# Output projection of two attention layers as seven products of halves, with its weights loaded into the place of the value weights

## The chip, the cores and the metric

The kernel runs on one NeuronCore of one Trainium2 chip. Five engines work side by side, each through its own queue of instructions in a fixed order: TensorE (PE in the profile, its weight loads PEld) multiplies matrices, VectorE (DVE), ScalarE (ACT) and GpSimd (POOL) work element by element, and SyncE (SP) issues most transfers (DMA). An instruction that has to wait holds up everything behind it in its own queue. Matrix products land in PSUM, eight banks of 128 x 512 float32 numbers; GpSimd takes no part in emptying them here, so VectorE and ScalarE carry every result out.

The metric is the device time of one execution, in microseconds (us): from the first to the last of the program's work, one launch.

## What is computed

Four layers in a row act on x of shape (2, 512, 32, 32), all in float32. Only the last two are touched by the change. Layers 2 and 3 are plain self-attention blocks over 1024 positions with 8 heads of 64 channels:

```python
xn = group_norm(x)                              # 8 groups in layer 2, 32 in layer 3
q, k, v = split(W_qkv @ xn + b_qkv)             # (2, 512, 1024) each
a = softmax(q.T @ k / 8) ; h = a @ v            # for each of 8 heads
x = x + W_proj @ h + b_proj                     # W_proj is 512 x 512
```

The two samples of the batch are called b = 0 and b = 1. Layer 0 (attention over sampled keys and an MLP) and layer 1 (linear attention) come before and take most of the time.

## The kernel before

x stays in SBUF through the whole program as eight tiles `x[b][t]` of 128 channels by 1024 positions (t = 0 to 3). Each of layers 2 and 3 is one call of `attention`, in three stages.

**Queries, keys, values** (`queries_keys_values`). The products with W_qk and W_v are made by Winograd's form of Strassen's scheme: both matrices are cut in four blocks, and seven products of block sums (P1 to P7, table `SEVEN`) take the place of eight. The sums of the weights (`left_sums`, four element-wise operations, on GpSimd) stand in a second tile beside the raw weights; the sums of the other side come from `right_sums`. A small comparison at the end, `oki`, says whether all logits are small, and every engine branches on it: with these inputs into `heads_bounded`.

**Heads** (`heads_bounded`). A unit is one sample b, one pair of heads p and one half h of the 512 + 512 query positions: 16 units of 8 steps, one step n for 128 keys. In a step, `score` makes four products into a score tile `s` (two banks, two buffers), ScalarE takes the exponential into `e` (six buffers), and `value`, two steps later, multiplies `e` with the values into the unit's result `o`. For the divisor the eight `e` are added up: three adds on GpSimd into `some`, the others on VectorE into `sum`. After a unit's last step ScalarE and VectorE carry `o` out of its banks into the queries' place (`q`), and four steps later `divide` makes the column sums `d` of `sum` on TensorE, takes the reciprocal on VectorE, multiplies, and adds the values' bias.

Only TensorE's order is written out by hand in this stage; the order of the other engines is what the framework's scheduler makes of the dependences. `o` and `d` have one place of two banks each. So the next unit may not start its `o` before the last one is carried out, and TensorE's hand-written order makes room for that: no `value` in the third step of a unit, two in the fourth (`for j in ([], [i - 3, i - 2])[i % NB == 3] if i % NB in (2, 3) else [i - 2]`).

**Projection** (end of `heads_bounded`, `project_block`, L591 to L609). For each sample and each block o of 128 output channels, eight products of 128 x 128 by 128 x 512 fill two banks `pb`, and two VectorE operations (L607) add the bias and the result to x. The last unit's `divide` stands after the first block. In layer 3 each half goes out at once with a DMA on SP's queue (L609). In layer 2 the statistics for layer 3's norm (`channel_means`, `group_means`) are taken in between, and the norm's first block (`norm_first`) is made before the last block.

The projection's weights are four tiles, loaded by SP after the branch (`projection_weights`, L943). The next layer's W_qk and W_v are loaded by SP as soon as the last value product of this layer has read the old ones. GpSimd has no work in the projection; in layer 2 it makes the sums of layer 3's W_qk in that time.

Of the kernel before, what the change touches and what calls it, by code (L numbers as in the profile page):

```python
# [11 lines left out]
F32 = mybir.dt.float32  # L12
# [40 lines left out]
class Net:  # L53
# [539 lines left out]
    def project_block(self, acc, att, w, bias: str, b: int, o: int, out):  # L593

        nc = self.nc
        for h in range(2):
            for t in range(CT):
                nc.tensor.matmul(  # L598
                    acc[:, h, :],
                    lhsT=w[t][:, o * P : (o + 1) * P],  # L600
                    rhs=att[t][:, h * HF : (h + 1) * HF],
                    start=(t == 0),
                    stop=(t == CT - 1),
                )
        for h in range(2):
            xt = self.xs[b][o][:, h * HF : (h + 1) * HF]
            nc.vector.scalar_tensor_tensor(xt, acc[:, h, :], self.col(bias, o), xt, ALU.add, ALU.add)  # L607
            if out is not None:
                nc.sync.dma_start(out[b, o][:, h * HF : (h + 1) * HF], xt)  # L609
# [321 lines left out]

    def attention_weights(self, pool, k: int):

        got = []
        for name in ("qk", "v"):
            src = self.io[f"l{k}_{name}"]
            got.append(pool.tile(list(src.shape), F32, tag=name, name=f"{name}w{k}"))
            self.nc.sync.dma_start(got[-1], src)  # L940
        return got

    def projection_weights(self, pool, k: int):  # L943
        got = []
        for t in range(CT):
            got.append(pool.tile([P, C], F32, tag=f"proj{t}", name=f"proj{k}{t}"))
            self.nc.sync.dma_start(got[-1], self.io[f"l{k}_proj"][t])
        return got

    def averages(self):  # L950
# [2 lines left out]
            self.avg[k] = self.norm.tile([P, P], F32, tag="avg", name=f"avg{k}")  # L953
            self.nc.sync.dma_start(self.avg[k], self.io[f"l{k}_avg"])

    def attention(self, k: int, weights, out, meanwhile=lambda: None):


        nc = self.nc
        with ExitStack() as ctx:  # L960
            one = self.pool(ctx, f"a{k}")
            ones = one.tile([P, DH], F32, tag="ones", name=f"ones{k}")
            nc.vector.memset(ones, 1.0)
            data = []
            for b in range(B):
                qs = [one.tile([P, N], F32, tag=f"q{b}{t}", name=f"q{k}{b}{t}") for t in range(CT)]
                ks = [one.tile([P, N], F32, tag=f"k{b}{t}", name=f"k{k}{b}{t}") for t in range(CT)]
                v = [one.tile([P, 2, C], F32, tag=f"v{b}{n}", name=f"v{k}{b}{n}") for n in range(NB // 2)]
                data.append((qs, ks, v))
            small_logits, got = self.queries_keys_values(k, weights, ones, data, meanwhile)  # L970
            if k == 2:
                self.means_tiles(3, 0)
                self.first[3] = self.first_block(3, 0)

            with self.tc.If(small_logits > 0) as cmp:
                self.heads_bounded(k, ones, data, out)
            with cmp.Else():
                self.heads_general(k, data)
                with ExitStack() as ctx2:
                    proj = self.projection_weights(self.pool(ctx2, f"a{k}_w_p"), k)  # L980
                    ps = self.pool(ctx2, f"a{k}_ps_p", 2, psum=True)
                    for b in range(B):
                        for o in range(CT):
                            acc = ps.tile([P, 2, HF], F32, tag="ps", name=f"pbg{k}{b}{o}")
                            self.project_block(acc, data[b][0], proj, f"pb{k}", b, o, out)
                    if k == 2:
                        for t in range(CT):
                            self.channel_means(3, 0, t)
                        for _ in self.group_means(3, 0, ps.tile([P, 2, HF], F32, tag="ps", name="gm3g")):
                            pass  # L990
                        self.norm_first(3)
            return got

    def queries_keys_values(self, k, weights, ones, data, meanwhile):

# [5 lines left out]
        with ExitStack() as ctx:  # L1003
# [133 lines left out]
                            for c in range(2):  # L1137
                                self.norm_block(k, 1, xns[1][i], i, c, act)
            with self.tc.manual_schedule(engines={mybir.EngineType.SP}):
                got = meanwhile()  # L1140
                reason = "a product of two comparisons"
                return nc.values_load(oki, min_val=0, max_val=1, skip_runtime_bounds_check_because=reason), got

    def largest(self, k, b, ones, cm, small, ps_g, flag):

# [71 lines left out]
        for c in range(2):  # L1217
            self.norm_block(k, 0, self.first[k], 0, c, (self.nc.vector, self.nc.scalar)[c])

    def heads_bounded(self, k, ones, data, out):  # L1220

# [2 lines left out]
        nc = self.nc  # L1226
        halves = [slice(0, DH), slice(DH, P)]
        with ExitStack() as ctx:
            proj = self.projection_weights(self.pool(ctx, f"b{k}_w"), k)
            ep = self.pool(ctx, f"b{k}_e", 6)  # L1230
            ap = self.pool(ctx, f"b{k}_a", 1)
            ap2 = self.pool(ctx, f"b{k}_a2", 2)
            ps_s = self.pool(ctx, f"b{k}_ps_s", 2, psum=True)
            ps_o = self.pool(ctx, f"b{k}_ps_o", 1, psum=True)

            def score(unit, n):
                b, p, h, state = unit
# [1 line left out]
                cut = slice(h * HF, (h + 1) * HF)  # L1239

                third = unit is units[0] and n == 2
                s = (ps_o if third else ps_s).tile([P, 2, HF], F32, tag="sd"[third], name=f"s{k}{b}{p}{h}{n}")
                for par, rows in enumerate(halves):
                    for c in range(2):
                        at = n * P + c * DH
# [20 lines left out]
            def value(unit, n):  # L1266
                b, p, h, state = unit
                v = data[b][2]
                if n == 0:
                    state["o"] = ps_o.tile([P, 2, HF], F32, tag="o", name=f"o{k}{b}{p}{h}")  # L1270
                o, e = state["o"], state["e"][n]
                for r, rows in enumerate(halves):
                    for par in range(2):
# [12 lines left out]

            def divide(unit):
                b, p, h, state = unit
                d = ps_o.tile([P, 2, HF], F32, tag="d", name=f"d{k}{b}{p}{h}")
                for r, rows in enumerate(halves):  # L1290
                    for par in range(2):
                        nc.tensor.matmul(
# [7 lines left out]
                nc.vector.tensor_tensor(res, res, t, ALU.mult)  # L1300
                nc.vector.tensor_scalar(res, res, self.col(f"vb{k}", p), None, ALU.add)

            units = [(b, p, h, {}) for b in range(B) for p in range(CT) for h in range(2)]
            steps = [(unit, n) for unit in units for n in range(NB)]
            with self.tc.manual_schedule(engines={mybir.EngineType.PE}):


                for i in range(len(steps) + 5):
                    if i < len(steps):
                        score(*steps[i])  # L1310
                    for j in ([], [i - 3, i - 2])[i % NB == 3] if i % NB in (2, 3) else [i - 2]:
                        if 0 <= j < len(steps):
                            value(*steps[j])
                    if i % NB == 4 and NB < i < len(steps):
                        divide(steps[i - NB][0])
                for b in range(B):
                    for o in range(CT):
                        acc = ps_s.tile([P, 2, HF], F32, tag="s", name=f"pb{k}{b}{o}")
                        self.project_block(acc, data[b][0], proj, f"pb{k}", b, o, out)
                        if b == o == 0:  # L1320
                            divide(units[-1])
                        if k == 2:
                            n = b * CT + o
                            if 1 <= n <= CT:
                                self.channel_means(3, 0, n - 1)
                            elif n == CT + 1:
                                steps = self.group_means(3, 0, ps_o.tile([P, 2, HF], F32, tag="d", name="gm3"))
                                next(steps)
                            elif n == CT + 2:
                                next(steps, None)  # L1330
                                self.norm_first(3)

    def heads_general(self, k, data):
        with ExitStack() as ctx:
# [78 lines left out]
def conv_seq_kernel(ctx: ExitStack, tc: tile.TileContext, io: dict[str, bass.AP], out: bass.AP):  # L1413
# [3 lines left out]
    with tc.tile_pool(name="w_at", bufs=1) as wpool, tc.tile_pool(name="norm", bufs=2) as norm:  # L1417
        net.norm = norm
        with tc.tile_pool(name="w_l1", bufs=1) as lpool:
            net.mlp0()  # L1420
            l1 = net.layer1_weights(lpool)
            l2 = net.attention_weights(wpool, 2)
            net.averages()
            net.layer1(*l1)
        l3 = net.attention(2, l2, None, lambda: net.attention_weights(wpool, 3))
        net.attention(3, l3, out.rearrange("b (t p) h w -> b t p (h w)", p=P))

# [7 lines left out]
def _blocks(w):  # L1437

    return np.ascontiguousarray(w.T).reshape(-1, P, w.shape[0])
# [38 lines left out]
def _layout(i):  # L1478
# [10 lines left out]
    def over(v):  # L1489
# [33 lines left out]
        "l1_b": np.concatenate([l1["bv"], l1["bq"], l1["bk"]]),  # L1523
        "l2_qk": _slabs(l2["qkv_w"][: 2 * C].T.reshape(1, C, 1, 2 * C))[0],
        "l2_v": _slabs(l2["qkv_w"][2 * C :].T.reshape(1, C, 1, C))[0],
        "l2_proj": _blocks(l2["proj_w"]),
        "l2_avg": _average(C // 8),
        "l3_qk": _slabs(w3[: 2 * C].T.reshape(1, C, 1, 2 * C))[0],
        "l3_v": _slabs(w3[2 * C :].T.reshape(1, C, 1, C))[0],
        "l3_proj": _blocks(l3["w_proj"]),  # L1530
        "l3_avg": _average(C // 32),
    }

# [15 lines left out]
```

## Time and profile before

| | us |
|---|---|
| median of 4 runs (3453.45 to 3454.75) | 3454.61 |
| the profiled execution | 3454.33 |
| its span, first to last instruction | 3452.5 |
| layers 0 and 1, and layer 2's queries, keys and values | 0 to 2704.5 |
| layer 2: heads / projection and way into layer 3 | 240.4 / 58.4 |
| layer 3: queries, keys and values | 147.9 |
| layer 3: heads / projection and end | 240.1 / 61.2 |

The stages are read from the timeline: the first score product of layer 2 starts at 2704.56 us, the first projection product at 2944.91, the first product of layer 3 at 3003.32, its heads at 3151.66 and its projection at 3391.28. TensorE is busy for 98% of the span, at a mean granted clock of 0.997. Lines of the profile read: start, duration, engine, line of the code, operation, output <- inputs, and in square brackets the idle time before it with what ended it. The profile counts every float32 product as two matrix records.

### The profile page before, as it was taken

Reading aid. Unit: us, or ns where it says so; the run is one execution under the profiler, and the core shown is the slowest. Engines: PE = TensorE matmul, PEld = TensorE weight load, DVE = VectorE, ACT = ScalarE, POOL = GpSimd, SP = SyncE. Lnnn points to the kernel's source line nnn. Section 1 sums busy time; section 2 is a strip of 40 time slices with the busy share of each in tenths; the row PEclk is TensorE's granted clock in tenths of the full one; section 3 lists DMA queues with packets and bytes.
Section 4 is the critical chain, followed back from the end, with each engine's and each line's share of the span. In section 5 each row is a group of like instructions: output and inputs, shape, how many; then the busy total and the mean of one; then the engine's idle time right before and its main releaser. Section 6 shows DMA issues by size and latency. Waiting matters only on the chain.

```text
span 3452.5 us, 60119 instructions
## 1 busy us (share of the span) xinstructions
PE 3397.1 (98%) x25280; PEld 1263.3 (37%) x25280; DVE 2314.5 (67%) x2539; ACT 2021.0 (59%) x2100; POOL 2080.1 (60%) x1584
## 2 busy tenths in 40 slices
PE   6999999999999999999999999999999999999999
PEld 2333333333333333333333334444555433455333
DVE  6877777777777567767776664575556577555774
ACT  5877877877887577877887761111111466113661
POOL 4778777787787577787788874342323444234441
PEclk9999999999999999999999999999989999999999
DMA  5778777777887577777788872111000100000001
GB/s 152 157 141 157 150 154 148 155 158 143 156 162 144 105 157 151 155 154 146 163 169 160 158 151 79 49 37 37 1 1 0 50 1 1 1 0 13 2 1 50
DMA packets 103247, 342.64 MB, mean 99 GB/s; under 512 B 12720, under 2 KB 14384, under 8 KB 100144
## 3 DMA queue, kind: packets, MB, share of 16 engines
q0 software_dynamic: 73296, 266.90, 40.9%
q1 hardware_dynamic: 28656, 69.68, 6.5%
q8 instruction: 202, 3.31, 0.4%
q10 hardware_dynamic: 1008, 2.06, 0.2%
q14 instruction: 85, 0.70, 0.1%
HBM read 67.27 MB, written 4.46 MB: 21 GB/s over the span
## 4 chain that ended last, share of the span: by engine, by line
PE 80%; DVE 15%; ACT 2%; POOL 1%; issue 1%; DMA 0%; DVEq 0%; ACTq 0%; SPq 0%; POOLq 0%
PE hp L486 46%; DVE h L455 3%; PE pb L598 3%; DVE r L1298 3%; PE sim L518 3%; PE o L1275 2%; DVE sum L1262 2%; PE s L1246 2%; PE qk20P L1041 1%; PE qk30P L1041 1%; PE m_0P L649 1%; PE qk31P L1041 1%; PE m_6P L649 1%; PE m_4P L649 1%; PE m_3P L649 1%; PE m_1P L649 1%
## 5 line engine op out<-in xcount | busy, mean ns | idle before, releaser
L486 PE MATMUL hp<-h,w 128*32 128x512 f32 x16384 | 1832.7, 593 | 5.4 <-DVE h L455 3.6
L455 DVE CUSTOM_DVE_ANT_1 h<-tx,bank 128x1024 f32<-128x1024 f32 x1024 | 1180.9, 1216 | 332.4 <-PE hp L486 309.3
L491 ACT ACTIVATE h<-hp,magb 128x1024 f32<-128x1024 f32 x1024 | 1124.0, 1113 | 416.2 <-PE hp L486 415.2
L486 PEld LDWEIGHTS hp<-h,w 128*32 128x32 f32 x16384 | 545.3, 110 | 1215.4 <-issue 1118.7
L478 POOL DMA_DIRECT2D h<-h x509 | 452.6, 1026 | 391.9 <-ACT h L497 334.6
L504 POOL TENSOR_TENSOR h<-h,h 128x1024 f32<-128x1024 f32 x255 | 613.7, 2407 | 21.3
L502 POOL TENSOR_SCALAR h<-h,flip 128x1024 f32<-128x1024 f32 x256 | 448.4, 1751 | 0.9 <-ACT h L491 0.9
L1250 ACT ACTIVATE e<-s 128x1024 f32<-128x1024 f32 x256 | 258.7, 1025 | 177.1 <-PE s L1246 164.4
L493 ACT ACTIVATE h<-h,flip 128x1024 f32<-128x1024 f32 x256 | 291.9, 1140 | 0.0
L1275 PE MATMUL o<-e,v 64*64 64x512 f32 x2048 | 261.0, 592 | 6.7 <-DVE q L1285 6.7
L1246 PE MATMUL s<-q,k 64*64 64x512 f32 x2048 | 259.8, 589 | 2.6 <-DVE v L1079 1.8
L1257 POOL TENSOR_TENSOR some<-some,e 128x1024 f32<-128x1024 f32 x64 | 151.5, 2367 | 75.7 <-ACT e L1250 73.4
L495 POOL TENSOR_SCALAR h<-h,flip 128x1024 f32<-128x1024 f32 x128 | 145.3, 1135 | 78.2 <-ACT h L491 77.0
L1255 POOL TENSOR_TENSOR some<-e,e 128x1024 f32<-128x1024 f32 x32 | 75.5, 2361 | 190.8 <-DVE sum L1264 155.6
L497 ACT ACTIVATE h<-h,flip 128x1024 f32<-128x1024 f32 x128 | 145.8, 1139 | 0.0
L518 PE MATMUL sim<-h,ends 128*32 128x512 f32 x1024 | 141.2, 592 | 0.0
L1260 DVE TENSOR_TENSOR sum<-e,e 128x1024 f32<-128x1024 f32 x32 | 46.3, 1448 | 136.1 <-ACT e L1250 136.1
L1275 PEld LDWEIGHTS o<-e,v 64*64 64x64 f32 x2048 | 75.7, 133 | 157.4 <-issue 123.7
L1246 PEld LDWEIGHTS s<-q,k 64*64 64x64 f32 x2048 | 78.5, 133 | 143.5 <-issue 116.6
L628 POOL TENSOR_TENSOR mlp_w<-mlp_w 128x512 f32<-128x512 f32 x16 | 22.5, 1405 | 160.7 <-DMA mlp_w<-in_mlp_w 106.4
L708 ACT ACTIVATE mh<-mh,cols 128x512 f32<-128x512 f32 x64 | 46.3, 724 | 124.1 <-DVE mh L726 65.4
L1029 POOL TENSOR_TENSOR sq<-q 128x512 f32<-128x512 f32 x32 | 33.3, 1039 | 139.3 <-DVE q L1048 95.2
(456 smaller groups left out, 3283.1 us busy)
## 6 DMA issues: line engine op xcount, KB each, us to landing
h<-h POOLq DMA_DIRECT2D x509, 512.0 KB, 6.5
lb<-logs SPq DMA_DIRECT2D x63, 512.0 KB, 5.2
mlp_w<-in_mlp_w SPq DMA_DIRECT2D x16, 1024.0 KB, 4.9
x<-in_x SPq DMA_DIRECT2D x8, 512.0 KB, 8.8
qkw<-in_l_qk SPq DMA_DIRECT2D x2, 2048.0 KB, 8.1
out<-x SPq DMA_DIRECT2D x16, 256.0 KB, 2.1
vw<-in_l_v SPq DMA_DIRECT2D x2, 1024.0 KB, 7.5
proj<-in_l_proj SPq DMA_DIRECT2D x8, 256.0 KB, 5.2
```

What stands on the lines that cost most here:

```text
L455: self.nc.vector._custom_dve(TENSOR_ADD_SAT, out=h[:, k, :, :], in0=x[:, jj, 2 * r + k, :].unsqueeze(1).to_broadcast([P, H, W]), in1=y[:, ...
L478: nc.gpsimd.dma_start(to, what, accum_op=ALU.add)
L486: nc.tensor.matmul(hp[rows, cut], lhsT=self.l0w2[:, 32 * q : 32 * q + 32], rhs=h1[k][:, cut], start=True, stop=True)
L491: nc.scalar.activation(y, hp, AF.Relu, bias=self.magb[:, q : q + 1])
L493: nc.scalar.activation(ys[0], ys[0], AF.Copy, scale=self.flip[:, 0:1])
L502: nc.gpsimd.tensor_scalar(y, y, self.flip[:, 2:3], 1.0, ALU.mult, ALU.mult)
L504: (nc.vector if final else nc.gpsimd).tensor_tensor(y, y, ys[2], ALU.add)
L518: nc.tensor.matmul(sims[u][at : at + 32, :], lhsT=self.ends[:, 28 - 4 * o : 60 - 4 * o], rhs=z[jj][:, h * HF : (h + 1) * HF], start=(o == ...
L649: self.nc.tensor.matmul(acc[p], lhsT=w[:, a, k, p * P : (p + 1) * P], rhs=right(r, k), start=k == 0, stop=k == 1)
L1246: nc.tensor.matmul(s[halves[c], par, :], lhsT=ks[p][rows, at : at + DH], rhs=qs[p][rows, cut], start=True, stop=True)
L1250: nc.scalar.activation(e, s, AF.Exp, scale=DH**-0.5)
L1275: nc.tensor.matmul(o[halves[par], r, :], lhsT=v[n // 2][rows, n % 2, at : at + DH], rhs=e[rows, par, :], start=(n == 0), stop=(n == NB - 1),)
```

## The change

In layers 2 and 3:

- The projection is made by the seven products too, per sample 28 products of 128 x 128 by 128 x 512 where there were 32. Its weights come in the layout of the other raw weights, one tile of 1 MB, with `left_sums` on GpSimd (`project_left`). The sums of the other side (`project_right`) are eight subtractions of 128 x 512 per sample: all on GpSimd for b = 0, half on GpSimd and half on VectorE for b = 1. They stand in buffers of `e`. The results are gathered as in the MLP: per sample 14 VectorE operations and 2 ScalarE copies that read PSUM, and 6 adds on GpSimd (L1334 of the new code).
- The projection's weights take the buffer of the value weights. SP loads them before the branch, once the last value product has read the old ones; layer 3's value weights are loaded after layer 2's projection.
- `o` and `d` of a unit share one place of two banks, and there are two such places, taken in turn by h. TensorE's order has one `value` in every step, always two steps behind.
- The last unit's `divide` stands after the third product (P1, P3, P2) of sample 0. The statistics for layer 3's norm are taken during sample 1, with `group_means` after its fourth and fifth product.

```diff
-    def projection_weights(self, pool, k: int):
-        ...
+    def attention_weights(self, pool, k: int, name: str):
+        src = self.io[f"l{k}_{name}"]
+        tag = "qk" if name == "qk" else "v"
+        got = pool.tile(list(src.shape), F32, tag=tag, name=f"{name}w{k}")
+        self.nc.sync.dma_start(got, src)
         return got
...
             with self.tc.manual_schedule(engines={mybir.EngineType.SP}):
-                got = meanwhile()
+                got = self.attention_weights(wpool, 3, "qk") if k == 2 else None
+                proj = self.attention_weights(wpool, k, "proj")
                 reason = "a product of two comparisons"
...
-            proj = self.projection_weights(self.pool(ctx, f"b{k}_w"), k)
+            wp = self.pool(ctx, f"b{k}_w", 1)
...
+            ps_even = self.pool(ctx, f"b{k}_ps_e", 1, psum=True)
             ps_s = self.pool(ctx, f"b{k}_ps_s", 2, psum=True)
-            ps_o = self.pool(ctx, f"b{k}_ps_o", 1, psum=True)
+            ps_odd = self.pool(ctx, f"b{k}_ps_o", 1, psum=True)
+
+            def place(h, name):
+                return (ps_even, ps_odd)[h].tile([P, 2, HF], F32, tag="o", name=name)
...
-                    state["o"] = ps_o.tile([P, 2, HF], F32, tag="o", name=f"o{k}{b}{p}{h}")
+                    state["o"] = place(h, f"o{k}{b}{p}{h}")
...
-                d = ps_o.tile([P, 2, HF], F32, tag="d", name=f"d{k}{b}{p}{h}")
+                d = place(h, f"d{k}{b}{p}{h}")
...
+            def project_left():
+                more = wp.tile([P, 3, 2, 2 * P], F32, tag="proj", name=f"projm{k}")
+                self.left_sums(nc.gpsimd, proj, more)
+                return [proj[:, i] for i in range(4)] + [more[:, i] for i in range(3)]
+
+            def project_right(b):
+                att = data[b][0]
+                r = [[att[2 * (i // 2) + c][:, (i % 2) * HF : (i % 2 + 1) * HF] for c in range(2)] for i in range(4)]
+                t = [ep.tile([P, 2, HF], F32, tag="e", name=f"pt{k}{b}{i}") for i in range(4)]
+                t1, t2, t3, t4 = ([x[:, c, :] for c in range(2)] for x in t)
+                for c in range(2):
+                    eng = nc.vector if b == 1 and c == 0 else nc.gpsimd
+                    eng.tensor_tensor(t1[c], r[1][c], r[0][c], ALU.subtract)
+                    eng.tensor_tensor(t2[c], r[3][c], t1[c], ALU.subtract)
+                    eng.tensor_tensor(t3[c], r[3][c], r[1][c], ALU.subtract)
+                    eng.tensor_tensor(t4[c], r[2][c], t2[c], ALU.subtract)
+                return [r[0], t3, r[2], r[3], t1, t2, t4]
...
+                for which in ("P1", "P3", "P2", "P6", "P7", "P5", "P4"):
+                    a, ri = SEVEN[which]
...
+                    acc = place(0, name) if which in ("P2", "P5") else ps_s.tile([P, 2, HF], F32, tag="s", name=name)
+                    for p in range(2):
+                        for c in range(2):
+                            nc.tensor.matmul(acc[:, p, :], lhsT=left[a][:, c, p * P : (p + 1) * P],
+                                rhs=right[ri][c], start=c == 0, stop=c == 1)
+                    for p in range(2):
...
+                        if which == "P1":
+                            nc.scalar.copy(u, got)
+                            add(vec, p, 0, got, True)
+                        elif which == "P3":
+                            add(vec, p, 1, got, True)
+                        elif which == "P2":
+                            add(vec, p, 0, got)
+                            store(p, 0)
+                        elif which == "P6":
+                            vec.tensor_tensor(u, got, u, ALU.add)
+                        elif which == "P7":
+                            vec.tensor_tensor(u3, got, u, ALU.add)
+                            add(pool, p, 3, u3)
+                            add(pool, p, 2, u3)
+                        elif which == "P5":
+                            vec.tensor_tensor(u, got, u, ALU.add)
+                            add(pool, p, 1, u)
+                            store(p, 1)
+                            add(vec, p, 3, got, True)
+                            store(p, 3)
+                        else:
+                            add(vec, p, 2, got, True)
+                            store(p, 2)
...
-                for i in range(len(steps) + 5):
+                for i in range(len(steps) + 2):
                     if i < len(steps):
                         score(*steps[i])
-                    for j in ([], [i - 3, i - 2])[i % NB == 3] if i % NB in (2, 3) else [i - 2]:
-                        if 0 <= j < len(steps):
-                            value(*steps[j])
+                    if i >= 2:
+                        value(*steps[i - 2])
                     if i % NB == 4 and NB < i < len(steps):
                         divide(steps[i - NB][0])
-                for b in range(B):
-                    for o in range(CT):
-                        ...
+                    if i == len(steps) // 2 + NB:
+                        left = project_left()
+                right = project_right(0)
+                for n, _ in enumerate(project(0, left, right)):
+                    if n == 2:
+                        divide(units[-1])
+                        right = project_right(1)
+                for n, _ in enumerate(project(1, left, right)):
+                    if k == 2:
+                        if n < 2:
+                            self.channel_means(3, 0, 2 * n)
+                            self.channel_means(3, 0, 2 * n + 1)
+                        elif n == 3:
+                            means = self.group_means(3, 0, place(1, "gm3"))
+                            next(means)
+                        elif n == 4:
+                            next(means, None)
+                            self.norm_first(3)
```

In `add`, the target is the half tile `x[b][2 * (i // 2) + p]`, half `i % 2`; `store` is the DMA of that half in layer 3.

## Prediction

> **What bounds the kernel now.** I read the page's busy shares and chain first, then the busy time by stage, then the timeline around three seams: between two units of the heads, at the heads' start, and through the projection.
>
> ```profile
> PE 3397.1 (98%) x25280; PEld 1263.3 (37%) x25280; DVE 2314.5 (67%) x2539; ACT 2021.0 (59%) x2100; POOL 2080.1 (60%) x1584
> 2704.50:2944.90 240.40, 236.31 (x2168) 81.21 (x2168) 164.71 (x137) 146.60 (x159) 113.59 (x48) 1.00 0.03 10
> 3151.20:3391.30 240.10, 236.09 (x2169) 82.24 (x2169) 164.72 (x138) 145.31 (x158) 113.42 (x48) 1.00 0.02 6
> ...
> 2931.46 1.90 PE L1246 MATMUL s<-q,k 64*64 64x512 f32 x16
> 2932.85 0.69 DVE L1285 TENSOR_TENSOR q<-o,q 128x512 f32<-128x512 f32 x1
> 2933.59 1.95 PE L1275 MATMUL o<-e,v 64*64 64x512 f32 x16 [0.23 <-DVE q L1285]
> ...
> 2703.76 0.33 SPq L940 DMA_DIRECT2D vw<-in_l_v  x1
> 2709.23 2.36 POOL L1255 TENSOR_TENSOR some<-e,e 128x1024 f32<-128x1024 f32 x1 [13.78 <-ACT e L1250]
> DMA to landing us min/median/max: 4.8/7.5/10.2
> ...
> 3391.36 7.06 PE pb L598 x16
> 3398.42 1.02 PE d L1292 x8
> 3399.44 48.28 PE pb L598 x112
> ...
> L607 DVE SCALAR_TENSOR_TENSOR x<-pb,cols,x 128x512 f32<-128x512 f32 x32 | 22.6, 747 | 67.6 <-PE pb L598 67.6
> L628 POOL TENSOR_TENSOR vm<-vw x2: 1299/1300/1300, 2572.7 to 3019.8; 128x512 f32<-128x512 f32 x2
> L764 POOL TENSOR_TENSOR x<-x,u 128x512 f32<-128x512 f32 x16 | 22.2, 1391 | 0.0
> L1298 DVE RECIPROCAL r<-r 128x512 f32<-128x512 f32 x32 | 107.3, 3353 | 1.1
> L1260 DVE TENSOR_TENSOR sum<-e,e 128x1024 f32<-128x1024 f32 x16 | 23.3, 1453 | 68.6 <-ACT e L1250 68.6
> L1264 DVE TENSOR_TENSOR sum<-sum,some 128x1024 f32<-128x1024 f32 x15 | 18.4, 1225 | 1.6
> 3448.52 0.99 SPq L609 DMA_DIRECT2D out<-x  x2
> ```
>
> The first three rows: TensorE is the bound, and in the heads it is busy for 236 of 240 us. But busy time counts the modelled end of a pipelined product. By the rate of issue (8 records in 0.86 us, so 0.1073 us each) the 2168 records of layer 2's heads fill 232.6 us: 7.8 are lost. The second group shows where: 16 score records from 2931.46 are issued by 2933.18, and the next `value` starts at 2933.59, 0.41 us later, when VectorE has carried the last unit's result out of its only place. That comes 15 times per layer. The third group is the weights' transfer at the heads' start and GpSimd's first add; the fourth the projection, products without a gap while L607 waits 67.6 us for them. The rest are prices.
>
> **The change, part by part** (minus is faster).
>
> *Two places for results.* A unit's first `value` no longer waits for the last unit's eviction; it has eight more steps. Layer 2: 7.8 less 1.06 at the start (the fourth score waits from 2707.13 to 2708.20 for the first exponential, behind a table load that stays) and some 0.2 at the ends leaves 6.5, or 15 x 0.43. Layer 3: 239.6 from first score to projection, less 2168 x 0.1073 and 0.1, leaves 6.9. Bounds: 30 x 0.41 = 12.3 and 13.4. What is late next? `d` shares the place and comes two steps after the eviction, 3.4 us of slack; exponentials take 1.03 of a step's 1.72. Nothing, so I take **-13.0**.
>
> *Eight products fewer per layer.* 128 records of the projection took 55.1 us in layer 3's chain (7.06 + 48.28 less the seams), 0.43 each, 0.858 per product. 2 x 8 x 0.858 = **-13.7** if nothing stalls.
>
> *Left sums.* Written in the middle of the heads, but in the compiled order GpSimd's first four instructions after the branch, in both layers; behind them stand all adds into `some`. They wait for the projection's weights, which SP issues at the same moment as `vw` above (the last value product is done) and which land 4.8 us later (the row's other transfer, 10.2, was queued behind the MLP's weights; here the queue is empty, so 4.8; far bound 10.2). Layer 2: landed at 2708.6, four sums at a pitch of 1.35 (starts 2572.71, 2574.09, 2575.44) to 2714.1, first `some` done at 2716.5 where it was 2711.6. The seventh exponential needs that buffer: it starts at 2716.55, not 2715.43, ends at 2717.6, and the ninth score, which needs its banks, was due at 2717.70. Cost 0. Layer 3 has no table load and runs 1.1 earlier against the weights (issue 3150.9): first `some` done 3163.6, seventh exponential done 3164.7, ninth score due 3163.70: **+1.0**. A transfer later by x costs about x in each layer.
>
> *Right sums of sample 0.* Eight GpSimd subtractions at 1.37 = 11 us, right behind its last add (2.3 us before the projection). The first one needed, for P6, is the fifth: done 4.6 us in, P6 is due at 11.2. Cost 0; it would take 6.6 us of delay.
>
> *The gathering.* From the first product (t = 0): P1, P3, P2 end at 10.3, `d` 11.2, P6 14.6, P7 18.0, P5 21.5, P4 24.9, P1 of sample 1 at 28.3. VectorE's compiled order puts the divisor's chain ahead of P6's eviction: P2's two adds and two statistics to 13.1, add 0.7, reciprocal 3.35, one right sum, the multiplication, one P6 eviction, the bias: 19.2. Only then can GpSimd go on with sample 1's right sums (they need the last unit's result): three at 1.37, to 23.3; behind them in its queue P7's four adds and P5's two, at the MLP's pitch of 1.22, to 30.6. VectorE in turn waits for these adds (x from P5, two statistics of finished halves), and behind those waits stand P4's two evictions: 31.2 and two of 0.7, done at 32.6. P3 of sample 1 uses P4's banks and was due at 28.3: a stall of 4.3 on TensorE in layer 2. Adds and subtractions of VectorE and GpSimd meet here; L1260, beside a busy GpSimd, takes 0.23 more than L1264. Two or three such meetings: I take **+5.0**; ends 3.5 (no meeting, pitch 1.2) and 9 (each of the nine GpSimd instructions as long as 1.73, the longest L628 of the MLP). Layer 3 has no statistics: chain done at 18.0, GpSimd's third subtraction and fourth add at 27.0, P4 evicted at 27.8, due 28.3: **+0.3** (0 to 3).
>
> The Trainium skill, SBUF — State Buffer, Who interferes with whom, speaks against this change more strongly: a VectorE instruction with two SBUF inputs and a GpSimd instruction that reads SBUF exclude each other for the whole instruction. This case's 1.453 against 1.225 us is a part of a GpSimd add's 2.36, so the trace shows the meeting but not the full lock. With every meeting at a full 1.3 us the stall in layer 2 would be about 7, and the sum 3437.3.
>
> *Way into layer 3.* Its first product waits for VectorE's last eviction, 1.45 us after the last projection product, as before; the norm's first block is ready 2 us ahead. The sums of W_qk (4 x 2.45), done under the projection before (from 2959.6), now follow GpSimd's last add: done about 12.8 us after the projection, first read at 15.3 (1.6 plus sixteen products of 0.858). Layer 3's value weights land 5 us in and are summed from 17 us, wanted at 50. Cost 0, at most 2 if GpSimd is late by 4. W_qk's own transfer stays where it was.
>
> *End.* After P7, four GpSimd adds, then two for P5: from the end of the last product minus 6.0 to plus 1.4. SP sends the halves in order, and behind the last add's store stand three more, 0.5 us each (two took 0.99): the last issue is at plus 2.9, where it was plus 1.45. **+1.4** (0.8 to 2.5).
>
> Sum: -13.0 - 13.7 + 1.0 + 5.0 + 0.3 + 1.4 = -19.0. The profiled execution took 3454.33 us (span 3452.5 and 1.8 around it), 0.3 below the median of 3454.61: **3435.3 us**.
>
> **Rivals.**
>
> *The weights land late.* For: one of two transfers of 1 MB took 10.2. Against: that one had the queue full. At the median of 7.5 the heads stall by 2.6 and 2.7 more: 3440.6; at 10.2, 3446.0. The Trainium skill's DMA: Bandwidth & Descriptors, Measured, has 6.15 us of transfer for 1 MB; by that the sum would be 3438.0.
>
> *A new wait takes the old one's place in the heads.* The gap at the seam closes, but exponential, `some` or `d` stalls as much. For: GpSimd waits 155.6 us for `sum` before its first add of a unit, so its chain follows VectorE's. Against: it has 5 us to spare before the seventh exponential. Then only the projection gains: 3448.3, within 0.2%.
>
> *GpSimd becomes the bound, and the kernel slower.* Its 27 instructions that TensorE, VectorE or the end wait for (nine per gathering, six at the end, three or so on the way into layer 3) cost about 27 us per us that each takes longer. The 19.0 of gain and the 6.9 of the bound are used up at 0.95 more, so from about 2.2 us for an operation of 128x512. For: 60% busy already, and its rows go up to 1.73. Against: means of 1.27 to 1.39 beside a working VectorE. At 2.4: about 3465.
>
> **How the numbers follow.** Forecast 0.67, late weights 0.17, a new wait 0.11, GpSimd the bound 0.05. A measurement here tells no less than 0.2% (6.9 us) from no change. Faster by more: 0.67 + 0.17 and a third of the new wait, 0.88; within: 0.08; slower: 0.04. The range: down to 3430 (no stall in layer 2, all of the 13.4), up to 3444 (weights at 7.5 with 3 us more of stall fall inside, a full new wait does not).
>
> **What would show it.** Products `pb` 224 records instead of 256; no wait of `value` for VectorE's `q`; GpSimd's first `some` at about 12 us into each layer's heads, and 1 us lost by TensorE in layer 3 there; in layer 2's projection one stall of some 5 us ahead of sample 1's P3, ended by VectorE's x; layer 2's projection about 55 us long, layer 3's 49.5; the last store 3 us after the last product. Wrong it is if the heads stay at 240 us, if P4 of sample 0 waits as well (VectorE held before P6's second eviction), or if layer 3's third product waits for GpSimd.

## The result: 0.18% faster, where 0.55% was forecast

The changed kernel takes 3447.91 us (median; 3443.51 to 3452.18), the one before 3454.16 in the same comparison: a ratio of 0.9982, 95% interval 0.9978 to 0.9987. That is 6.3 us where 19 were forecast: slower than the forecast range (3430 to 3444). The interval is clear of 1, but the gain is under the 0.2% that the prediction set as the least it could tell from no change. The profiled execution took 3447.59 us (span 3445.5), 6.74 less than the one before.

The first line of the page, changed kernel:

```profile
PE 3380.6 (98%) x25248; PEld 1257.8 (37%) x25248; DVE 2393.5 (69%) x2579; ACT 2026.2 (59%) x2108; POOL 2171.6 (63%) x1640
```

Busy time by stage, changed kernel: stretch and length, then busy time and count of PE, PEld, DVE, ACT and POOL, the granted clock, DMA share and GB/s. The stretches are layer 2's heads, its projection up to layer 3's first product, layer 3's heads, its projection up to the last product:

```profile
2703.90:2938.60 234.70, 233.22 (x2168) 82.74 (x2168) 181.27 (x135) 148.06 (x159) 127.53 (x54) 1.00 0.02 6
2938.60:3001.90 63.30, 53.79 (x129) 22.92 (x125) 48.35 (x68) 6.21 (x10) 32.45 (x23) 0.95 0.02 4
3150.20:3384.90 234.70, 232.99 (x2168) 83.46 (x2168) 180.73 (x136) 146.78 (x158) 127.52 (x53) 1.00 0.02 6
3384.90:3437.70 52.80, 49.94 (x124) 21.24 (x120) 37.21 (x44) 3.45 (x6) 31.56 (x23) 1.00 0.14 51
```

The 32 matrix records fewer (25280 to 25248) are the 16 products. From the first score product to the first projection product the heads are 5.6 and 4.9 us shorter; 12.0 in all was forecast (13.0 less 1.0 for the left sums). But layer 2's projection with the way into layer 3, 58.4 us before and forecast at about 56.5 (55 and the way), now takes 63.3: with eight products less it is five microseconds longer. Layer 3's takes 52.8 where it took 56.4 and 49.5 was forecast, and from the last product to the end of the span pass 7.8 us, not 4.8. Where TensorE waited, from layer 2 on (total, times, longest):

```profile
PE pb21P L1352 <- DVE x L1332: 4.2, 1, 4.2
PE d L1293 <- DVE q L1286: 3.0, 2, 2.5
PE s L1247 <- ACT e L1251: 2.3, 2, 1.7
...
PE pb31P L1352 <- DVE x L1332: 1.2, 1, 1.2
PE pb30P L1352 <- DVE x L1332: 1.1, 1, 1.1
PE pb20P L1352 <- DVE x L1332: 1.1, 1, 1.1
```

`value` waits for `q` no more; the first row is sample 1's P3, the stall that was forecast at 5. The second row, the divisor's wait, and the last two, P6's, were not forecast at all. The timeline shows what stands behind them (start, duration, engine, line, operation, idle time before and its end):

```profile
2940.96 4.49 DVE L1263 TENSOR_TENSOR sum<-sum,e 128x1024 f32<-128x1024 f32 x2
2942.12 2.25 POOL L1320 TENSOR_TENSOR pt<-q,pt 128x512 f32<-128x512 f32 x1
2944.33 2.24 POOL L1322 TENSOR_TENSOR pt<-q,pt 128x512 f32<-128x512 f32 x1
2945.55 2.10 DVE L1265 TENSOR_TENSOR sum<-sum,some 128x1024 f32<-128x1024 f32 x1
...
2950.92 0.68 DVE L1286 TENSOR_TENSOR q<-o,q 128x512 f32<-128x512 f32 x1
2951.65 1.09 PE L1293 MATMUL d<-sum,ones 64*64 64x512 f32 x8 [2.48 <-DVE q L1286]
2953.80 8.80 PE L1352 MATMUL pb20P<-pt,projm 128*128 128x512 f32 x16 [1.06 <-DVE x L1332]
...
2977.08 5.40 PE L1352 MATMUL pb21P<-q,projm 128*128 128x512 f32 x8 [4.18 <-DVE x L1332]
```

Two things are to be seen. VectorE's adds, 1.22 us alone, and GpSimd's subtractions for sample 0, 1.3 alone, run turn by turn, 2.25 us each, so the eviction (L1286) that frees the divisor's banks comes 12.3 us after the first product. And behind the long waits 16 records take 8.80 us and 8 take 5.40, where the same shapes take 7.03 and 3.60 elsewhere: TensorE runs at half pace for a while. The granted clock is 0.50 from 2955 to 2957 us and from 2979 to 2981, and 0.95 over the whole stage.

My theory after this reading: the two places gave their full gain; VectorE and GpSimd shut each other out at the start of the projection; the waits that follow make TensorE slow as well; and the old order of GpSimd's work does the rest. The rivals: the heads gave part back themselves; it is the order of VectorE's instructions; the slow products have a cause of their own.

### The profile page after: what moved, and what is told of

It is laid out like the page before. It is cut to its first block, busy times and chain, and to the rows that moved or that the text cites. A ratio compares the mean times of both kernels' runs of the same rounds, so it can differ in the third digit from the quotient of the medians.

```text
span 3445.5 us, 60176 instructions
## 1 busy us (share of the span) xinstructions
PE 3380.6 (98%) x25248; PEld 1257.8 (37%) x25248; DVE 2393.5 (69%) x2579; ACT 2026.2 (59%) x2108; POOL 2171.6 (63%) x1640
## 4 chain that ended last, share of the span: by engine, by line
PE 86%; DVE 9%; POOL 2%; ACT 1%; issue 1%; DMA 0%; ACTq 0%; DVEq 0%; POOLq 0%; SPq 0%
PE hp L486 46%; PE s L1247 6%; PE o L1276 6%; DVE h L455 3%; PE sim L518 3%; PE qk20P L1034 1%; PE qk30P L1034 1%; PE m_0P L649 1%; PE m_6P L649 1%; PE m_4P L649 1%; PE m_3P L649 1%; PE m_1P L649 1%; PE qk31P L1034 1%; PE qk21P L1034 1%; PE m_5P L649 1%; PE m_2P L649 1%
## 5 line engine op out<-in xcount | busy, mean ns | idle before, releaser
L1258 POOL TENSOR_TENSOR some<-some,e 128x1024 f32<-128x1024 f32 x64 | 163.7, 2558 | 26.4 <-ACT e L1251 23.0
L1261 DVE TENSOR_TENSOR sum<-e,e 128x1024 f32<-128x1024 f32 x32 | 72.2, 2256 | 89.8 <-ACT e L1251 89.8
L1299 DVE RECIPROCAL r<-r 128x512 f32<-128x512 f32 x32 | 107.3, 3353 | 1.1
```

## The experiments

**Two places alone.** The kernel before with this edit and its old projection:

```diff
-    state["o"] = ps_o.tile([P, 2, HF], F32, tag="o", ...)
+    state["o"] = place(h, ...)          # and d, gm3, the third score tile
-    for j in ([], [i - 3, i - 2])[i % NB == 3] if i % NB in (2, 3) else [i - 2]:
+    if i >= 2: value(*steps[i - 2])
```

> The kernel before with one part of the change alone: two places in turn for results and divisors, one value product in every step; the projection stays as it was, eight products and no work for GpSimd. Theory A (the heads gain what was forecast, and the new projection gives it back): the seams' waits of 6.5 and 6.8 us go in layers 2 and 3, nothing else changes, 3454.2 - 13.3 = 3441, which is 7 below the whole change (3447.9). Rival B (the heads give back by new waits of their own, so that the change as a whole cannot gain more): 3448 or more, with TensorE waiting in the middle of units. In both the adds `sum` stay above 1.5 us each, since GpSimd's `some` now falls on them.

Measured: 3440.34 us (before: 3453.64), ratio 0.9958 (0.9941 to 0.9975). The whole gain is 13.3 us, and the two stages of heads account for it (6.5 and 6.9 us shorter). The only waits of TensorE left in them are layer 2's first exponential (0.8 us) and 0.9 at the start of each. The adds `sum<-e,e` take 2.38 us on average, 1.45 before, without any cost. Rival B falls. So all of the change that touches the projection *loses* 7.6 us.

**Sample 0's right sums left out.** The kernel leaves the eight subtractions out; raw halves stand in their place.

```diff
+    if b == 0:
+        return [r[0], r[1], r[2], r[3], r[0], r[1], r[2]]
```

> The changed kernel without the eight subtractions of sample 0's right sums (raw halves take their place in its products P6, P7, P5, P4, so its x is wrong). Theory A (VectorE and GpSimd exclude each other, and the subtractions hold VectorE's last adds): the three `sum` adds at the end of the heads fall from 2.25, 2.25, 2.10 to about 1.25 each, the divisor's wait for `q` (2.48 us in layer 2, 0.51 in layer 3) and the wait of P6 (1.06) go, and with them the slow products behind them (1.8); sample 1's P3 then waits some 2 us longer, since the chain behind the divisor is as long as it was: -4, about 3444. Rival B (VectorE's order does it: its subtractions for sample 1 stand ahead of the last unit's eviction whatever GpSimd does): the divisor still waits 2 us or more in layer 2, 3447 to 3448.

Measured: 3439.14 us, ratio 0.9957 (0.9940 to 0.9973), 8.8 below the changed kernel. VectorE at the same place:

```profile
2939.55 1.22 DVE L1263 TENSOR_TENSOR sum<-sum,e 128x1024 f32<-128x1024 f32 x1
...
2942.11 1.22 DVE L1263 TENSOR_TENSOR sum<-sum,e 128x1024 f32<-128x1024 f32 x1
...
2943.85 1.22 DVE L1265 TENSOR_TENSOR sum<-sum,some 128x1024 f32<-128x1024 f32 x1
...
2949.11 1.09 PE L1293 MATMUL d<-sum,ones 64*64 64x512 f32 x8
```

All three adds are back at 1.22 and the divisor waits for nothing, though here all four of VectorE's subtractions for sample 1 stand ahead of the eviction, two more than in the changed kernel: rival B falls. Twice as much was gained as expected. In layer 2 P3's wait did not grow (3.9 us), because the divisor's chain behind VectorE's backlog had moved forward with the rest, and in layer 3 the waits of P6 and P3 (1.07 and 1.25 us) went too.

**The same sums made in the heads**, one per unit, nothing left out:

```diff
+    t1, t2, t3, t4 = ([x[:, c * HF : (c + 1) * HF] ...] for x in data[0][1])    # the keys' place
...
+    if len(steps) // 2 <= i < len(steps) and i % NB == 6:
+        right_early((i - len(steps) // 2) // NB)
```

> The changed kernel with sample 0's right sums made in the heads of sample 1, one subtraction on GpSimd per unit behind its last add, in the place of sample 0's keys; GpSimd's order is written by hand, everything else is computed as before. Theory A: the projection as without these sums (about -4), and in the heads nothing, since GpSimd has some 7 us without work in each unit: about 3444. Rival B (each subtraction meets a VectorE add in the heads and TensorE pays): up to 8 x 1.2 us per layer come back, 3448 to 3463.

Measured: 3439.35 us, ratio 0.9953 (0.9936 to 0.9969). The eight subtractions cost the heads nothing (234.6 and 234.5 us, where the changed kernel has 234.7 twice), and layer 3's projection, whose divisor, P6 and P3 no longer wait, takes 49.6 us from the first product to the end of the last.

**Filling the waits with products done over again**, first too many, then fewer:

```diff
+    again = {(0, "P2"): 5, (1, "P1"): 8}.get((b, which), 0) if k == 2 else 0     # second run: 3 and 5
+    for n in range(again):
+        nc.tensor.matmul(acc[:, 0, :], lhsT=left[a][:, 0, 0:P], rhs=right[ri][0], start=True, stop=True)
```

> The changed kernel with more work for TensorE: in layer 2's projection five products are made once more ahead of sample 0's P2 (2.15 us, into P2's own bank) and eight ahead of sample 1's P1 (3.43 us), so that most of the two long waits (2.48 and 4.18 us) is filled. Theory A (the products behind each wait run at half pace because TensorE had been idle): both waits shrink to under 1 us, the products behind them run at 0.43 us from the first, and the kernel is about 3.6 us faster for doing 13 products more: 3444.3. Rival B (the half pace comes from something else, the engines that read the same banks for one): the products behind stay slow, 3447.9. Rival C (the fill pushes the work behind it): slower, up to 3453.

> The changed kernel with three products once more ahead of sample 0's P2 and five ahead of sample 1's P1 in layer 2 (at 0.858 us each 2.57 and 4.29 us; e4_fill had taken 0.43 for a product, so its fill was twice what was written). Theory A (TensorE runs at half pace for some microseconds after an idle time of over 2 us, at 1.8 us a time): both waits go, nothing else is delayed, and eight more products make the kernel 3.4 us faster than the changed one: about 3444.5. Rival B (the idle time costs only itself, and the slow products have another cause): 3447.9.

Measured: 3447.49 us (0.9982; 0.9973 to 0.9992) and 3446.00 us (0.9979; 0.9969 to 0.9988), neither told apart from the changed kernel by the total. The stage tells more: from layer 2's first projection product to layer 3's first it is 63.3 us in the changed kernel, 62.9 with 13 products more (11.2 us of work) and 61.6 with eight more (6.9). Of the first fill:

```profile
2953.26 7.13 PE L1357 MATMUL pb20P<-pt,projm 128*128 128x512 f32 x16
...
2977.41 3.60 PE L1357 MATMUL pb21P<-q,projm 128*128 128x512 f32 x8
```

The same products that took 8.80 and 5.40 us take 7.13 and 3.60, with the same readers of their banks at work, and the stage's granted clock is 1.00 in both runs (0.95 in the changed kernel): the half pace comes from TensorE's idle time, some 1.7 to 1.8 us a time. The second run gained 1.7 us in that stage and not 3.4, since short waits (1.0, 0.4, 0.95 us) stayed where the fill now ended too early.

The profile of the first fill also shows one reason why its total says little. In layer 3, where nothing was filled, the divisor waited 2.52 us and P6 1.06, and slow products followed:

```profile
3396.63 1.09 PE L1293 MATMUL d<-sum,ones 64*64 64x512 f32 x8 [2.52 <-DVE q L1286]
3398.78 8.80 PE L1357 MATMUL pb30P<-pt,projm 128*128 128x512 f32 x16 [1.06 <-DVE x L1332]
```

The changed kernel's profile has 0.51 and 1.07 us and then 7.10 for the same instructions. This projection was 2.2 us longer than there (54.9 and 52.75 us). So the length of this stall is not fixed by the code: it differs between two profiles of the same instructions, and what decides it was not tested.

**GpSimd's adds ahead of its subtractions for sample 1**, on top of the sums in the heads:

```diff
+    if c == 1: yield [...]                               # in project_right, between the two halves
...
     if n == 2:
         divide(units[-1])
-        right = project_right(1)
+        sums = project_right(1); right = next(sums)      # VectorE's half
+    elif n == 5:
+        next(sums, None)                                 # GpSimd's half, behind P7's and P5's adds
```

> As e3_right0_early (3439.4), and in GpSimd's order the six adds of P7 and P5 of sample 0 stand ahead of its four subtractions for sample 1, which are needed only 13 us later. Theory A (what holds sample 1's P3 in layer 2 is GpSimd's queue: three subtractions that wait for the divisor, and behind them the adds that VectorE needs before it may empty P4): the adds start when P7 is summed, 2.5 us earlier, the wait of 4.43 us falls to about 1.5, and the slow products behind it (6.18 us for eight records where 3.60 is the rule) run at full pace: -5.5, about 3434. Rival B (the statistics on VectorE or the pace of the adds hold it): the wait stays above 3.5 and the slow products with it, 3438 to 3439.

Measured: 3433.90 us, ratio 0.9942 (0.9926 to 0.9957). The gain over the run before is 5.5 us, as expected by theory A: sample 1's P3 in layer 2, first with the sums in the heads alone, then with the adds ahead, waits 0.67 us where it waited 4.43, and no slow products follow.

```profile
2971.91 6.18 PE L1365 MATMUL pb21P<-q,projm 128*128 128x512 f32 x8 [4.43 <-DVE x L1345]
...
2970.91 3.70 PE L1366 MATMUL pb21P<-q,projm 128*128 128x512 f32 x8 [0.67 <-DVE x L1346]
```

**The left sums one per unit**, on top of that:

```diff
-    left = project_left()
+    lefts = project_left()               # now yields after each of its four sums
...
+    if i % NB == 6 and i < 4 * NB:
+        left = next(lefts)
```

> As e5_adds_first, and the four left sums of the projection's weights are made one per unit, behind GpSimd's last add in each of the first four units, where they had stood together ahead of its first add. Theory A (the waits of 0.72 us in layer 2 and 1.74 us in layer 3 some 12 us and 9 us into the heads are the price of that place): both go, -2.5 against e5_adds_first, about 3431.5. Rival B (a left sum that meets VectorE's adds in the middle of the heads costs as much there): no change against e5_adds_first.

Measured: 3430.62 us, ratio 0.9934 (0.9919 to 0.9949); on another chip 3430.66 (0.9939; 0.9926 to 0.9953), against this expectation:

> The same kernel as e6_left_spread once more, on the same chip as e9_end: 3430 to 3431.

3.3 us go. Both waits of `s` for `e` in the heads' first unit are gone, and the four stages of the first table read:

```profile
2702.90:2936.80 233.90, 233.00 (x2169) 82.87 (x2169) 183.16 (x135) 148.18 (x159) 137.95 (x60) 1.00 0.02 6
2936.80:2989.50 52.70, 50.26 (x128) 21.70 (x125) 41.62 (x68) 6.25 (x10) 19.93 (x16) 1.00 0.02 4
3137.90:3370.70 232.80, 232.80 (x2169) 98.54 (x2169) 180.84 (x136) 146.82 (x158) 136.58 (x60) 1.00 0.02 6
3370.70:3420.20 49.50, 49.48 (x120) 21.25 (x120) 31.76 (x43) 3.52 (x6) 18.47 (x16) 1.00 0.15 55
```

This version beats both kernels, by 22.9 us (before) and 17.3 us (changed).

**VectorE's projection in an order by hand**, and another order of the last products:

```diff
-    with self.tc.manual_schedule(engines={PE, Pool}):
+    with self.tc.manual_schedule(engines={PE, Pool, DVE}):      # the projection alone
...
     elif n == 5:
+        sums = project_right(1)      # VectorE's and GpSimd's halves, ahead of P4's evictions
```

> As e6_left_spread, with two more changes of order: in the projection VectorE's order is written by hand (the divisor's chain and P4's evictions ahead of the statistics), and in the last sample of layer 3 the products go P1, P3, P6, P7, P5, P4, P2, so that finished halves come out two at a time to the end. Theory A: layer 2's last wait of some 1.5 us before sample 1's P3 goes, and the end, 7.8 us from the last product's end to the last store landed since six stores of 0.25 MB are issued in the last 3.4 us, falls to about 5: -4.5 against e6_left_spread, about 3427, and about 7.8 of the 13.7 us of the eight products fewer per layer beyond what the two places give (3440.3). Rival B (the last transfers take as long wherever they are issued): -1.5, 3430.

Measured: 3443.23 us, ratio 0.9969 (0.9957 to 0.9981): 12.6 us *worse* than the kernel it was to improve. In my order VectorE's four subtractions for sample 1 fall beside GpSimd's four:

```profile
2964.29 1.64 DVE L1340 TENSOR_TENSOR pt<-q,pt 128x512 f32<-128x512 f32 x1
2965.35 1.71 POOL L1339 TENSOR_TENSOR pt<-q 128x512 f32<-128x512 f32 x1
2965.86 1.75 DVE L1341 TENSOR_TENSOR pt<-q,q 128x512 f32<-128x512 f32 x1
```

They take 0.69 us on VectorE and 1.27 on GpSimd when alone; here both take about 1.7 each. P4's evictions stand behind them, so P3 waits 3.6 us in both layers with slow products behind (5.40 and 5.25 us), and layer 3's first products wait 3.0 and 1.6. The new order of the last products took about 1 us off the end (6.9 where it was 7.8), not the 2.8 expected. I had made the change's own mistake again.

**The end**: the last sample's products in two other orders, VectorE's order left alone.

```diff
-    for which in ("P1", "P3", "P2", "P6", "P7", "P5", "P4"):
+    for which in ("P1 P3 P6 P7 P5 P4 P2" if last else ...).split():      # second run: "P1 P2 P6 P7 P4 P5 P3"
...
-    nc.sync.dma_start(out[b, o][:, cut], ...)
+    (nc.sync, nc.scalar)[p].dma_start(out[b, o][:, cut], ...)            # first run alone
```

> As e6_left_spread (3430.6), VectorE's order as there, and two changes at the end alone: in the last sample of layer 3 the products go P1, P3, P6, P7, P5, P4, P2, and the stores of the second block of each pair are issued on ScalarE's queue in place of SP's. Theory A (the end is 3 us longer than before the change because the last six stores, 1.5 MB, are issued within 3.4 us and take 4.2 us at 378 GB/s): with two halves left to store after the last product the time from its end to the end of the span falls from 7.8 to about 5, -2.5, about 3428. Rival B (the end is set by something behind the stores): it stays at 7 or more, 3430.

> As e6_left_spread (3430.7), and in the last sample of layer 3 the products go P1, P2, P6, P7, P4, P5, P3: one quarter of the sample is finished early, one by P4, one by P5 and the last by P3, two stores each, all on SP's queue. In e9_end eight stores (2 MB) were still to come after P5. Theory A (the end is as long as the bytes that are left when the last products run): four stores leave while TensorE still works, 0.5 MB is left after the last product, and from its end to the end of the span it takes some 5.5 us in place of 7.8: 3428.5. Rival B (fixed): 7 or more, 3430.5.

Measured: 3430.03 us (0.9934; 0.9920 to 0.9947) and 3429.86 us (0.9928; 0.9914 to 0.9941), not told apart from 3430.66. From the last product to the end of the span it is 6.9 and 7.5 us where it was 7.8. In the second the last store is issued 1.6 us after the last product and lands 2.2 later, but the span goes on for 3.7 us, 2.3 of them a wait of SP for TensorE's sequencer. What sets the end then is left open; by rival B it is something behind the stores, and the new orders are worth about a microsecond at most.

## Why the prediction was wrong, point by point

Against the sum of -19.0, the profiled executions differ by -6.74. The stages (changed kernel less kernel before, less what was forecast) miss by +0.9 and +0.6 (heads, with the 13.0 taken as 6.5 for each layer), +6.7 (layer 2's projection), +2.9 (layer 3's) and +1.6 (end). The earlier layers happened to be 0.7 shorter, and the time outside the span 0.3 longer. That adds up to the difference of 12.3.

- **Two places, -13.0: right.** Alone they give 13.3. The rival of a new wait in the heads is refuted with it: that its 3448.3 us lies beside the measured 3447.9 is chance, for the heads did gain and the projection lost.
- **Eight products fewer per layer, -13.7: right as a term.** Without stalls layer 3's projection is the 49.5 us that were forecast.
- **"Right sums of sample 0 ... Cost 0": the step that failed.** I priced them by when P6 needs them, and never asked what their run does to VectorE, whose last `sum` adds stand in the same microseconds. The divisor was set down at 11.2 without a wait. It waited 2.48 and 0.51 us and P6 1.06 and 1.07, and layer 2 paid 1.8 more in slow products.
- **"The meeting but not the full lock": wrong.** The Trainium skill, SBUF — State Buffer, Who interferes with whom, says that a VectorE instruction with two SBUF inputs contends with a GpSimd instruction that reads SBUF, and that the one that has the shared ports keeps them to its end. Here 1.22 became 2.25 beside 1.3, and the slowest `sum` add took 3.21, its own 1.22 and 2.0 of the 2.36 that GpSimd's add lasts. The mean of 1.453 that I read as a weak meeting was one of adds that mostly fell between GpSimd's: 28 of the 32 overlapped one by some 0.35 us and took 0.2 longer. Even with that rule my sum was 3437.3, since I applied it to the gathering alone.
- **The gathering, +5.0 and +0.3: the place and the cause were right** (GpSimd's adds behind its subtractions, VectorE behind the adds; moving the adds removed it). The waits were 4.18 and 1.25 us; with the stalls ahead of it gone, layer 2's was 4.43, and the sum had given 4.3. Missing was the half pace behind a wait, 1.80 us.
- **Left sums, 0 and +1.0: too low by 0.6 and 0.7.** The weights landed in 4.77 us as forecast. But in layer 2 the first `some`, behind them, met VectorE's first `sum<-e,e` (in layer 3 the last left sum did, 2.16 us in place of 1.30):

```profile
2712.42 2.10 DVE L1261 TENSOR_TENSOR sum<-e,e 128x1024 f32<-128x1024 f32 x1 [8.67 <-ACT e L1251]
...
2713.40 3.34 POOL L1256 TENSOR_TENSOR some<-e,e 128x1024 f32<-128x1024 f32 x1
...
2716.77 1.94 ACT L1251 ACTIVATE e<-s 128x1024 f32<-128x1024 f32 x2 [2.74 <-POOL some L1256]
```

  With 3.34 us in place of 2.36 it ends 12.85 us into the heads (from 2703.89), not 11.9 as forecast (12.83 in layer 3), and the margin of 0.1 us was none. TensorE waited 0.6 us in layer 2 and 1.7 in layer 3.
- **End, +1.4: 3.0.** The last issue was forecast 2.9 us after the last product, and it stood there (3440.6). I had left out that six stores then follow each other within 3.4 us, and they land later. Time from issue to landing, changed kernel (min, median, max):

```profile
DMA to landing us min/median/max: 2.0/2.9/3.9
```

  The kernel before had 2.7 at most. But this can be only a part of the 1.6 us that were missed: in the second order tried for the end no store took more than 2.8 us, and the end was still 7.5. The rest stays open.
- **Way into layer 3, 0 to 2:** the first product waits 1.8 us, 0.2 more than before. **Weights late**, and **GpSimd the bound:** refuted, the first by 4.77 us, the second by a kernel that is not slower and by GpSimd's 32 busy of 63 us, though its subtractions did reach the 2.2 us that this rival named, beside VectorE's adds.

Of the changed kernel's 17.3 us above the best order that was run, the runs give 8.6 to sample 0's right sums at the end of the heads, with all that follows from them, 5.5 to GpSimd's order of adds and subtractions, and 3.3 to the place of the left sums.

## What to carry to other kernels

An instruction that is off the critical path still has a price where it slows another engine's: lay out, microsecond by microsecond, what runs on VectorE and GpSimd at the same time, and where both take two inputs from SBUF price the overlap at nearly the sum of both (here 2.25 us of 1.22 and 1.3, 1.7 of 0.69 and 1.27). Put such work where both have slack (here, one subtraction per unit of the heads), and ahead of an add that somebody waits for put nothing that itself waits. Forecast a long stall of TensorE with its slow restart: here waits of 3.6 us and more cost 1.6 to 2.6 us on top, and so did 2.48 and 1.06 us close together (1.7).

## What the runs showed of the hardware that was not expected

- VectorE's and GpSimd's 128x512 subtractions, 0.69 and 1.27 us alone, both took 1.6 to 1.75 side by side, a little under the sum of 1.96. VectorE's operations with one input from PSUM (0.74 us) kept their time beside a busy GpSimd.
- After idle times of 3.6, 3.9, 4.2 and 4.4 us TensorE's next eight records took 5.40, 5.18, 5.40 and 6.18 us, where 3.60 is the rule; after 2.48 and 1.06 us with only the divisor between them 16 took 8.80 for 7.03. After single waits of 1.25, 1.8 and 3.03 us nothing was slow (after the last, in the run with VectorE's order by hand, 32 records took 13.97 us at a clock of 1.00). The Trainium skill, TensorE: Matmul & The Clock Gate, Part 1, has half the clock after an idle window of about 3.4 us until about as much busy time has passed; the single waits agree. The pair of 2.48 and 1.06 us, neither of them that long, does not follow from it, and still the clock fell to 0.50. Doing eight products more in the waits made that stage 1.7 us shorter.
